# Transposed node table built before the main loop, and a new split of the gathered rows, in a graph message-passing kernel

## The chip, the cores and the metric

The kernel runs on one core of a Trainium2 chip. The metric is the time of one execution on the device, in microseconds (us). Five engines work side by side, each with its own queue of instructions: TensorE (PE in the profile, PEld for its weight loads), VectorE (DVE), ScalarE (ACT), GpSimd (POOL) and SyncE (SP), which here only issues DMA transfers. They wait for one another through semaphores.

## The reference

For 12500 nodes with 48 numbers each and 400000 edges (sorted by destination), one layer of message passing with a residual:

```python
h   = maximum(layernorm(x), 0)                    # [12500, 48]
tmp = concatenate([h[dst], h[src], edge_attr], 1) # [400000, 48 + 48 + 32]
msg = relu(tmp @ W1 + b1) @ W2 + b2               # [400000, 128] -> [400000, 48]
out = x + segment_sum(msg, dst, 12500)
```

The kernel never builds `tmp`. It forms two tables of node rows, `tab_a = h @ W1[:48] + b1` and `tab_b = h @ W1[48:96]`, both [12544, 128] in DRAM, and adds for each edge the row of its destination (from `tab_a`), the row of its source (from `tab_b`) and `edge_attr @ W1[96:]`. Since W2 is linear, the relu outputs are summed by destination first, and W2 is applied to the sums.

## The kernel before, in words

**Tiles and chunks.** 128 edges are a tile, 3125 tiles in all; 8 tiles (1024 edges) are a chunk, 391 chunks. Since edges are sorted by destination, the destinations of a chunk lie in a window of 80 nodes. 12 chunks share one accumulator of 1024 nodes in SBUF, a segment (`seg`, two of them in turn).

**Stage one, `node_tables`.** The node rows are loaded in six slices, normalised (DVE and ACT), transposed on PE into `ht` (features on partitions), and multiplied by the weights: first all of `tab_b`, then all of `tab_a`, each slice copied out of PSUM by ACT and DVE and stored by SP. Meanwhile POOL gathers the raw x rows of the source nodes of the first four chunks (`RAW = 4`; `gather`, line 760), because `tab_b` isn't ready that early; those rows are normalised too.

**Stage two, `windows`, the main loop.** The order of work on each engine is written out by hand (line 501 on). In iteration c:

- SP issues the loads of chunk c (`prepare`): edge attributes into `lhs` (line 354), the destinations broadcast over 80 partitions into `row` (356), the 80 rows of `tab_a` into `rhs` (364), whose address is first loaded into a register (272); then single rows of `tab_b` into `gs` (`rows`, line 289).
- POOL gathers source rows from `tab_b` by indirect DMA into `gb`, one tile of 128 rows an instruction (371). `gb` has 7 buffers.
- DVE compares `row` with the window's node numbers into the one-hot part of `lhs` (379), adds the sums of chunk c-2 to its segment (460), and builds the one-hot matrix `hot` (389).
- PE multiplies `lhs` by `rhs` for chunk c-1 (400), adds the source rows to it (421), and, for chunk c-2, sums the relu outputs by destination with `hot` (445).
- ACT does the relu of chunk c-1 (437).

**Three ways to a source row.** Not all source rows come through POOL. A second way are columns: `bt`, the table `tab_b` turned so that its 128 hidden values lie on partitions, stays in SBUF, and DVE and ACT copy one column of it per edge into `gt` (`columns`, line 348); PE turns `gt` back as it adds it. The addresses of the columns are loaded from SBUF into registers of the copying engine, in parts (`PARTS`; line 272). 143 columns a chunk are copied, 71 by DVE in five parts and 72 by ACT in six. The third way are the single rows that SP loads, 15 a chunk. As soon as 128 columns or rows are together they replace one of POOL's gathers.

**The turned table** `bt` is built in the first five chunks of the main loop (`turn`, lines 302 and 307): three blocks a chunk, each two products on PE and one copy on ACT. Columns therefore begin with chunk 5.

**Segments.** Every 12 chunks DVE copies the 80 overlapping nodes into the other segment and clears the rest of it (`segment_next`, 476 and 478); PE multiplies the finished segment by W2 in two blocks (488, 489), DVE adds it to x (495) and SP stores it (499), two chunks into the next segment. SP's store waits for DVE's addition, and everything SP issues behind it waits too.

Of the kernel before, what the change touches and what calls it, by code (L numbers as in the profile page):

```python
# [8 lines left out]
F32 = mybir.dt.float32  # L9
# [31 lines left out]
RAW = 4  # L41
NRAW = RAW * T
RAW_PART = 16
# [8 lines left out]
TURNS = 3  # L52
BLOCKS = (NPAD + CE - 1) // CE
BUILD = (BLOCKS + TURNS - 1) // TURNS
COLS = BUILD
# [10 lines left out]
STRIP = 144  # L66
# [3 lines left out]
RPART = 15  # L70
# [3 lines left out]
SEG0 = 161696  # L74
# [3 lines left out]
AT_PLACE, AT_SEG, SEG, NEXT = 16, 17, 18, 19  # L78
WIDTH = 20
# [10 lines left out]
BYCOLS = tiles_of(COLS, PART)  # L90
COLS_OF = {c: [j for j, of in enumerate(BYCOLS) if of == c] for c in sorted(set(BYCOLS))}
BYROWS = tiles_of(ROWS0, RPART)
EPS = 1e-5

# [7 lines left out]
def node_tables(nc, tc, keep, x, ident, w1, b1, wb, ht, xg, ones, tab_a, tab_b, index, loads,  # L102
                squares, most, check):

    slices = [(0, 8), (8, 16), (24, 20), (44, 20), (64, 20), (84, 14)]
# [6 lines left out]
    with ExitStack() as es:  # L112
        node = es.enter_context(tc.tile_pool(name="node", bufs=3))
        sqp = es.enter_context(tc.tile_pool(name="sqp", bufs=2))
        ps_t = es.enter_context(tc.tile_pool(name="ps_t", bufs=3, space=PSUM))
        ps_n = es.enter_context(tc.tile_pool(name="ps_n", bufs=3, space=PSUM))
# [5 lines left out]
        wa = keep.tile([2 * D + 1, 2, HID], F32, name="wa")  # L122
        nc.vector.memset(wb, 0.0)
# [21 lines left out]
        sqs = {}  # L145

        def centre(j):
            r0, rb = slices[j]
            h = xs[j]
            of = total[:, r0 : r0 + rb]  # L150
            nc.vector.tensor_reduce(of, h, AX.X, ALU.add)
            nc.vector.scalar_tensor_tensor(
                h, of.unsqueeze(2).to_broadcast([P, rb, D]), -1.0 / D, h,
                op0=ALU.mult, op1=ALU.add,
            )
            sqs[j] = sqp.tile([P, rb, D], F32, name="sq")
            nc.scalar.activation(sqs[j], h, AF.Square)

        def scale(j):
            r0, rb = slices[j]  # L160
            h = xs[j]
            of = rstd[:, r0 : r0 + rb]
            var = node.tile([P, rb], F32, name="var")
            nc.vector.tensor_reduce(var, sqs.pop(j), AX.X, ALU.add)
            std = node.tile([P, rb], F32, name="std")
            nc.scalar.activation(std, var, AF.Sqrt, bias=eps, scale=1.0 / D)
            nc.vector.reciprocal(of, std)
            nc.vector.tensor_mul(h, h, of.unsqueeze(2).to_broadcast([P, rb, D]))

        def turn(j):  # L170
            r0, rb = slices[j]
            h = xs[j]
            for g in range(0, rb // 2, 4):
                n = min(4, rb // 2 - g)
                p_t = ps_t.tile([2 * D, 4, P], F32, name="p_t")
                for q in range(n):
                    nc.tensor.transpose(
                        p_t[:, q, :],
                        h[:, 2 * (g + q) : 2 * (g + q) + 2, :].rearrange("p r d -> p (r d)"),
                        ident,  # L180
                    )
                nc.scalar.activation(
                    ht[: 2 * D, r0 // 2 + g : r0 // 2 + g + n, :], p_t[:, :n, :], AF.Relu
                )

        def table(j, wt, tv, dve):

            r0, rb = slices[j]
            rows = wt.shape[0]
            t = node.tile([P, rb, HID], F32, name="tab")  # L190
            for g in range(0, rb // 2, 2):
                n = min(2, rb // 2 - g)
                p_n = ps_n.tile([P, 2, 2 * HID], F32, name="p_n")
                for q in range(n):
                    nc.tensor.matmul(  # L195
                        p_n[:, q, :], ht[:rows, r0 // 2 + g + q, :],
                        wt.rearrange("k a h -> k (a h)"), start=True, stop=True,
                    )
                to = t[:, 2 * g : 2 * (g + n), :].rearrange("p r h -> p (r h)")
                of = p_n[:, :n, :].rearrange("p q h -> p (q h)")  # L200
                if dve and g % 4:
                    nc.vector.tensor_copy(to, of)
                else:
                    nc.scalar.copy(to, of)
            nc.sync.dma_start(tv[:, r0 : r0 + rb, :], t)

        for i in range(ns + 3):
            if i < ns:
                centre(i)
            if 0 <= i - 1 < ns:  # L210
                scale(i - 1)
            if 0 <= i - 2 < ns:
                turn(i - 2)
            if i == ns:
                squares()
            if i == ns + 1:
                most()
            if i == ns + 2:
                check()
            if 0 <= i - 3 < ns:  # L220
                table(i - 3, wb, tb_v, i >= ns)
        late = {1: (centre, ns), 2: (scale, ns), 3: (centre, ns + 1), 4: (scale, ns + 1)}
        for j in range(ns):
            if j in late:
                of, k = late[j]
                of(k)
            table(j, wa, ta_v, True)
# [707 lines left out]
```

## Time and profile before

| | |
|---|---|
| median of three runs | 3368.91 us |
| lowest, highest | 3366.3, 3372.81 us |
| profiled execution | 3372.65 us |
| its span | 3370.8 us |
| TensorE clock granted, mean | 0.911 |

The page of the profile gives, for one execution, the busy time of each engine, the chain of work that ended last, the costliest groups of instructions and the DMA traffic. "Issue" in it is time in which an engine waited for nothing that the profile shows. An instruction that only loads registers or issues a DMA isn't counted as busy; a `q` behind an engine's name (`SPq`, `DVEq`) marks such work of its queue. In the order of time each line has the start, the duration, the engine, the line of the code, what is written from what, and how many instructions are merged in it.

### The profile page before, as it was taken

The numbers are of one execution on the slowest core, as the hardware profiler recorded it, in microseconds if no ns is written. First come the engines' busy times: TensorE is split into PE (matmuls) and PEld (weight loads), VectorE is DVE, ScalarE is ACT, GpSimd is POOL, SyncE is SP. The second block draws the span as 40 slices with busy tenths as digits, with TensorE's granted clock in tenths as the row PEclk, the third lists the DMA queues.
The fourth block names the chain that finished last, engine by engine and source line by source line (L and its number), as shares of the span: only waits on it lengthen the run. The fifth ranks groups of instructions, "written<-read, shape, count | busy, mean of one in ns | idle before, by whom it ended". The sixth has DMA issues, their size and how long they took to land.

```text
span 3370.8 us, 115212 instructions
## 1 busy us (share of the span) xinstructions
PE 2775.6 (82%) x16394; PEld 2158.3 (64%) x16394; DVE 2800.1 (83%) x29140; ACT 3035.6 (90%) x28179; POOL 2530.0 (75%) x2670
## 2 busy tenths in 40 slices
PE   7987778888888888888887788888788788788777
PEld 6666666666666666666666666676666666666565
DVE  6588888888888888888888888888888888888876
ACT  5799998999998999998899999889998999999987
POOL 7677777777777777777777777777777777777776
PEclk9999998998898998988889999888998999899989
DMA  7433333333333333333333333333333333333333
GB/s 262 122 97 104 100 97 100 99 101 100 100 99 100 95 100 102 100 101 97 100 98 101 100 100 102 95 101 97 102 99 98 97 100 98 104 100 97 99 96 83
DMA packets 200234, 349.24 MB, mean 104 GB/s; under 512 B 69219, under 2 KB 107749, under 8 KB 198181
## 3 DMA queue, kind: packets, MB, share of 16 engines
q0 software_dynamic: 84800, 172.53, 18.9%
q1 hardware_dynamic: 114258, 169.09, 16.7%
q14 instruction: 634, 5.19, 0.5%
q8 instruction: 138, 2.26, 0.3%
q10 hardware_dynamic: 404, 0.17, 0.0%
HBM read 322.05 MB, written 22.07 MB: 102 GB/s over the span
## 4 chain that ended last, share of the span: by engine, by line
DVE 71%; issue 14%; PE 5%; DVEq 4%; POOL 2%; DMA 2%; ACT 0%; SPq 0%; POOLq 0%; ACTq 0%
DVE gt L348 47%; DVE lhs L379 12%; DVE hot L389 8%; DVEq L272 4%; DVE seg L460 2%; POOL gb L371 2%; PE pre L400 1%; PE p_g L445 1%; DVE xseg L495 1%; DVE seg L476 1%; DMA row<-in_dst 1%; PE p_f L488 1%; PE p_f L489 1%; DMA gb<-tab_b,srci 1%; PE p_n L195 1%
## 5 line engine op out<-in xcount | busy, mean ns | idle before, releaser
L371 POOL DMA_INDIRECT gb<-tab_b,srci x2618 | 2489.4, 951 | 812.7 <-issue 724.4
L348 ACT COPY gt<-bt 128x1 f32 x27705 | 2618.0, 188 | 63.9 <-issue 54.6
L348 DVE COPY gt<-bt 128x1 f32 x27335 | 1842.1, 144 | 463.3 <-issue 435.1
L400 PEld LDWEIGHTS pre<-rhs,lhs 112*128 112x128 f32 x6250 | 823.5, 208 | 277.1 <-issue 193.4
L400 PE MATMUL pre<-rhs,lhs 112*128 112x128 f32 x6250 | 841.5, 292 | 98.3 <-issue 56.7
L445 PE MATMUL p_g<-hot,hid 128*128 128x80 f32 x6250 | 794.0, 282 | 131.2 <-ACT hid L437 129.1
L445 PEld LDWEIGHTS p_g<-hot,hid 128*128 128x128 f32 x6250 | 758.4, 198 | 164.4 <-ACT hid L437 161.6
L421 PE MATMUL pre<-gb,ident 128*128 128x512 f32 (+2 forms) x1548 | 771.2, 627 | 34.3 <-DMA gb<-tab_b,srci 26.5
L437 ACT ACTIVATE hid<-pre 128x1024 f32<-128x1024 f32 x391 | 397.5, 1017 | 220.2 <-PE pre L421 205.8
L379 DVE TENSOR_SCALAR_CACHE_REDUCE lhs<-row,bw 80x1024 f32<-80x1024 int16 x391 | 494.6, 1265 | 14.8 <-DMA row<-in_dst 14.5
L421 PEld LDWEIGHTS pre<-gb,ident 128*128 128x128 f32 x1548 | 311.8, 225 | 281.0 <-issue 261.7
L421 PE MATMUL pre<-ident,gt 128*128 128x128 f32 x860 | 214.9, 336 | 261.7 <-DVE gt L348 234.7
L421 PEld LDWEIGHTS pre<-ident,gt 128*128 128x128 f32 x860 | 143.8, 210 | 291.5 <-issue 136.4
L389 DVE TENSOR_TENSOR hot<-wnum,rel 128x640 f32<-128x640 f32 x391 | 318.2, 814 | 0.0
L460 DVE TENSOR_TENSOR seg<-seg,p_g 128x160 f32 x391 | 121.5, 311 | 47.8 <-PE p_g L448 47.8
L448 PE MATMUL p_g<-ident,deg 80*128 80x80 f32 x782 | 156.4, 283 | 0.0
L448 PEld LDWEIGHTS p_g<-ident,deg 80*128 80x128 f32 x782 | 123.6, 198 | 0.0
L488 PE MATMUL p_f<-seg,w2s 128*48 128x512 f32 (+1 forms) x134 | 82.2, 700 | 44.3 <-DVE xseg L495 43.9
L489 PE MATMUL p_f<-seg,b2s 1*48 1x512 f32 (+1 forms) x134 | 76.2, 650 | 0.0
L488 PEld LDWEIGHTS p_f<-seg,w2s 128*48 128x48 f32 x134 | 12.3, 135 | 85.9 <-DVE xseg L495 60.0
L476 DVE MEMSET seg<- 128x944 f32 x64 | 54.1, 845 | 9.3
L489 PEld LDWEIGHTS p_f<-seg,b2s 1*48 1x48 f32 x134 | 11.3, 122 | 65.2 <-issue 65.2
(76 smaller groups left out, 429.0 us busy)
## 6 DMA issues: line engine op xcount, KB each, us to landing
gs<-tab_b SPq DMA_DIRECT2D x5760, 0.5 KB
row<-in_dst SPq DMA_DIRECT2D x390, 160.0 KB
lhs<-in_edge_t SPq DMA_DIRECT2D x390, 128.0 KB
gb<-tab_b,srci POOLq DMA_INDIRECT x2618
rhs<-tab_a SPq DMA_DIRECT2D x391, 40.0 KB
xseg<-in_x_t SPq DMA_DIRECT2D x33, 192.0 KB
out_x<-xseg SPq DMA_DIRECT2D x33, 192.0 KB
tab_b<-tab SPq DMA_DIRECT2D x3, 1280.0 KB
```

Of the source, the lines that this page charges most:

```text
L272: return nc.values_load_multi_w_load_instructions(table[c % P : c % P + 1, c // P, at : at + n], engines=[engine], min_val=0, max_val=1 << 23,
L348: copy(gts[j][:, e : e + 1], bt8[:, bass.ds(of, 4)].bitcast(F32))
L371: nc.gpsimd.indirect_dma_start(out=gb[:, t, :], out_offset=None, in_=tab_b[:, :], in_offset=bass.IndirectOffsetOnAxis(ap=srci[:, c * T + t ...
L379: nc.vector.tensor_scalar(lhs[:W, : n * P], row[:, : n * P], bw[:, c : c + 1], None, op0=ALU.is_equal, op1=ALU.add, accum_out=deg[:, :1],)
L389: nc.vector.tensor_tensor(hot[:, :n, :], wnum.unsqueeze(1).to_broadcast([P, n, W]), rel[:, c * T : c * T + n].unsqueeze(2).to_broadcast([P ...
L400: nc.tensor.matmul(pre[:, t, :], s["lhs"][:K, t * P : (t + 1) * P], s["rhs"][:K, :], start=t % BANK == 0, stop=False, skip_group_check=True,)
L421: nc.tensor.matmul(pre[:, t:e, :], lhsT, rhs, start=False, stop=True, skip_group_check=True)
L437: nc.scalar.activation(h[:, :n, :], s["pre"][:, :n, :], AF.Relu)
L445: nc.tensor.matmul(p_g[:, 0, :], s["h"][:, t, :], s["hot"][:, t, :], start=t == 0, stop=t == n - 1)
L448: nc.tensor.matmul(p_g[:, 1, :], s["deg"], ident[:W, :W], start=True, stop=True)
L460: nc.vector.tensor_add(to, to, s["p_g"])
L488: nc.tensor.matmul(p_f[:, :n], w2s, seg[:, 0, s], start=True, stop=False)
```

## The change

Seven things change together.

1. `bt` is built in stage one, for each slice before its rows of `tab_b` (`turned`); the rows of `tab_b` are then transposes of `bt` on PE, copied mostly by DVE (`back`). `tab_a` still comes from products with `ht` (`product`). The steps of a slice are cut into small functions and interleaved with the normalisation (`together`). `turn` is gone from the main loop, and `ht` lives in stage one alone.
2. A column of `bt` now stands at `(node mod 98) * 128 + node // 98`, the order in which the blocks come out, so the addresses are worked out in more DVE operations (`addresses`).
3. Five chunks use raw x rows (`RAW = 5`): 40 early gathers instead of 32. Columns begin in iteration 4.
4. 72 columns a chunk on DVE, in four parts of 23, 16, 17 and 16; 76 on ACT, in five parts; 17 single rows on SP. The place of the sums is loaded with the first part.
5. The segments are cleared by a DMA from a block of zeros, issued by SP behind the store of the segment (`segment_clear`), not by DVE.
6. `gb` has 8 buffers instead of 7.
7. The check that no edge lies outside its window uses a maximum and a minimum on DVE instead of squares on ACT; small operations for it move from POOL to DVE.

```diff
-RAW = 4
+RAW = 5
-RAW_PART = 16
+RAW_PART = 20
+RAW_EARLY = 16
-COLS = BUILD
+COLS = RAW - 1
 PARTS = (
-    (True, 0, 8), (True, 8, 15), (True, 24, 16), (True, 40, 20), (True, 60, 12),
-    (False, 72, 12), (False, 84, 8), (False, 92, 8), (False, 100, 20), (False, 120, 12),
-    (False, 132, 12),
+    (True, 0, 23), (True, 24, 16), (True, 40, 17), (True, 60, 16),
+    (False, 76, 12), (False, 88, 16), (False, 104, 20), (False, 124, 12), (False, 136, 16),
 )
-RPART = 15
+RPART = 17
...
+        def turned(j, g):
 
             r0, rb = slices[j]
+            n, at = min(2, rb // 2 - g), r0 // 2 + g
+            p_b = ps_n.tile([P, 4 * HID], F32, name="p_b")
+            parts = p_b[:, : 2 * n * P].rearrange("h (k q p) -> h k q p", k=2, q=n)
+            for k in range(2):
+                nc.tensor.matmul(
+                    parts[:, k, :, :].rearrange("h q p -> h (q p)"), wb[:, k, :],
+                    ht[: 2 * D, at : at + n, :].rearrange("k g p -> k (g p)"),
+                    start=True, stop=True,
+                )
+            nc.scalar.copy(
+                bt[:, 2 * at * P : 2 * (at + n) * P].rearrange("h (q k p) -> h q k p", k=2, q=n),
+                parts.rearrange("h k q p -> h q k p"),
+            )
+
+        def back(j, g):
+
+            r0, rb = slices[j]
+            n = min(4, rb - 2 * g)
+            if g == 0:
+                tabs[j] = node.tile([P, rb, HID], F32, name="tab")
+            p_n = ps_n.tile([P, 4 * HID], F32, name="p_n")
+            for q in range(n):
+                at = (r0 + 2 * g + q) * P
+                nc.tensor.transpose(p_n[:, q * HID : (q + 1) * HID], bt[:, at : at + P], ident)
+            copy = nc.scalar.copy if j >= ns // 2 and g % 6 == 4 else nc.vector.tensor_copy
+            copy(tabs[j][:, 2 * g : 2 * g + n, :].rearrange("p r h -> p (r h)"), p_n[:, : n * HID])
+            if 2 * g + n == rb:
+                nc.sync.dma_start(tb_v[:, r0 : r0 + rb, :], tabs.pop(j))
...
-        def turn(i):
-
-            n = min(T, NR - i * T)
-            p_t = ps_p.tile([P, T, HID], F32, name="pre")
-            parts = p_t.rearrange("h (k q) p -> h k q p", k=2)
...
         def segment_next(g):
 
             old, new = segs[g % 2], segs[(g + 1) % 2]
-            if g > 0:
-                for k in range(2):
-                    nc.vector.memset(new[:, k, W:], 0.0)
...
+        def segment_clear(g):
+
+            nc.sync.dma_start(segs[g % 2][:, :, W:], zeros.unsqueeze(0).to_broadcast([P, 2, L - W]))
...
                 if g > 0 and k == STORE:
                     segment_store(g - 1, L)
+                    if begin(g + 1) < NCH:
+                        segment_clear(g - 1)
...
-                for i in range(c * TURNS, min((c + 1) * TURNS, BLOCKS)):
-                    turn(i)
...
-    gp = ctx.enter_context(tc.tile_pool(name="gp", bufs=7))
+    gp = ctx.enter_context(tc.tile_pool(name="gp", bufs=8))
...
+            def lanes():
+                nc.vector.tensor_scalar(
+                    at, cols, 1.0 / NR, 0.5 / NR - 0.5, op0=ALU.mult, op1=ALU.add
+                )
+                nc.vector.tensor_scalar_add(at, at, ROUND)
+
+            def whole():
+                nc.vector.tensor_scalar(
+                    at, at, -ROUND, 4.0 - 4.0 * NR * P, op0=ALU.add, op1=ALU.mult
+                )
+                nc.vector.tensor_scalar_add(at, at, float(BT0))
+
+            def turned_places():
+                nc.vector.scalar_tensor_tensor(
+                    cols, cols, 4.0 * P, at, op0=ALU.mult, op1=ALU.add
+                )
+                nc.vector.tensor_scalar_add(at_place, place, float(BT0))
```

More of the change, by code (lines that the diff above doesn't have):

```diff
@@ L93 @@
 EPS = 1e-5
+ROUND = 1.5 * 2**23
 G = 5
@@ L99, with node_tables @@
 GNACC = 4
-def node_tables(nc, tc, keep, x, ident, w1, b1, wb, ht, xg, ones, tab_a, tab_b, index, loads,
-                squares, most, check):
-    slices = [(0, 8), (8, 16), (24, 20), (44, 20), (64, 20), (84, 14)]
+def node_tables(nc, tc, keep, x, ident, w1, b1, bt, wb, xg, ones, tab_a, tab_b, index, loads,
+                flags, check, addresses):
+    slices = [(0, 8)] + [(r0, 18) for r0 in range(8, NR, 18)]
     ns = len(slices)
@@ L188, in table @@
+        def turned(j, g):
             r0, rb = slices[j]
[L189 to L204, printed above, removed]
@@ L210, in node_tables @@
             if 0 <= i - 1 < ns:
[L211 to L227, printed above, removed]
+                side += scale(i - 1)
@@ new lines, in node_tables @@
+            if i >= ns:
+                side += later[i - ns]
+            main = [lambda g=g: turn(i - 2, g) for g in groups(i - 2, 4)]
+            t, b = groups(i - 3, 2), groups(i - 4, 2)
+            for k in range(max(len(t), len(b))):
+                if k < len(t):
+                    main.append(lambda g=t[k]: turned(i - 3, g))
+                if k < len(b):
+                    main.append(lambda g=b[k]: back(i - 4, g))
+            if main:
+                together(main, side)
+            else:
+                for do in side:
+                    do()
@@ L522, in windows @@
                     nc.vector.memset(segs[c], 0.0)
+                columns(c, 2)
                 columns(c, 3)
```

250 lines of the change are left out of this document (143 added, 107 removed).

## The prediction

> **What bounds the kernel now.** I read the page's parts 1, 4 and 5 first, then the waits of each engine, then the order of time in the steady part. On the page no engine is idle enough to be ruled out:
>
> ```profile
> span 3370.8 us, 115212 instructions
> PE 2775.6 (82%) x16394; PEld 2158.3 (64%) x16394; DVE 2800.1 (83%) x29140; ACT 3035.6 (90%) x28179; POOL 2530.0 (75%) x2670
> ...
> DVE 71%; issue 14%; PE 5%; DVEq 4%; POOL 2%; DMA 2%; ACT 0%; SPq 0%; POOLq 0%; ACTq 0%
> ...
> L371 POOL DMA_INDIRECT gb<-tab_b,srci x2618 | 2489.4, 951 | 812.7 <-issue 724.4
> L348 ACT COPY gt<-bt 128x1 f32 x27705 | 2618.0, 188 | 63.9 <-issue 54.6
> L348 DVE COPY gt<-bt 128x1 f32 x27335 | 1842.1, 144 | 463.3 <-issue 435.1
> ...
> L476 DVE MEMSET seg<- 128x944 f32 x64 | 54.1, 845 | 9.3
> ```
>
> The busy shares mislead. POOL is 75% busy, but with its issue time it is full: a gather starts every 1.25 us to the end (3349.74, 3350.98, 3352.23), and it waited for a buffer only once for long.
>
> ```profile
> 3349.74 0.94 POOL L371 DMA_INDIRECT gb<-tab_b,srci  x1 [0.30 <-issue]
> 3350.98 0.94 POOL L371 DMA_INDIRECT gb<-tab_b,srci  x1 [0.30 <-issue]
> 3352.23 0.94 POOL L371 DMA_INDIRECT gb<-tab_b,srci  x1 [0.30 <-issue]
> ...
> POOL gb L371 <- PE pre L421: 13.0, 1, 13.0
> ```
>
> The chain runs through DVE, 71%, with 14% "issue". Those gaps stand where DVE's queue loads column addresses into registers (line 272): the shortest load, of 8 values, takes 598 ns and the longest, of 20, 1352, so 63 ns a value. DVE begins its compare of line 379 once a chunk:
>
> ```profile
> L379 DVE TENSOR_SCALAR_CACHE_REDUCE lhs<-row,bw x287: 1259/1266/1276, 601.3 to 2995.0; 80x1024 f32<-80x1024 int16 x144
> ...
> L272 DVEq TENSOR_LOAD <-cols x7: 598/1100/1352, 2004.2 to 2013.3; - x7
> L272 SPq TENSOR_LOAD <-last x2: 557/862/1168, 2006.0 to 2012.6; - x2
> ```
>
> (2995.0 - 601.3) / 286 = 8.37 us a chunk. POOL needs 8 - (143 + 15) / 128 = 6.77 gathers a chunk, 8.46 us, and has a lead from the start. The two are level.
>
> SP does not appear in part 1, as issuing DMAs is not counted as busy. Yet its queue is a fourth loop of almost the same length. From the order of time on SP:
>
> ```profile
> 1068.32 0.33 SPq L354 DMA_DIRECT2D lhs<-in_edge_t  x1
> 1068.70 0.41 SPq L356 DMA_DIRECT2D row<-in_dst  x1
> 1070.47 0.33 SPq L364 DMA_DIRECT2D rhs<-tab_a  x1
> 1070.90 4.81 SPq L289 DMA_DIRECT2D gs<-tab_b  x15
> 1075.82 0.33 SPq L354 DMA_DIRECT2D lhs<-in_edge_t  x1
> ...
> 1137.97 0.33 SPq L354 DMA_DIRECT2D lhs<-in_edge_t  x1
> 1138.34 0.41 SPq L356 DMA_DIRECT2D row<-in_dst  x1
> 1140.08 0.33 SPq L364 DMA_DIRECT2D rhs<-tab_a  x1
> 1140.53 5.18 SPq L289 DMA_DIRECT2D gs<-tab_b  x15
> 1156.59 0.35 SPq L499 DMA_DIRECT2D out_x<-xseg  x1
> 1157.04 0.37 SPq L354 DMA_DIRECT2D lhs<-in_edge_t  x1
> ...
> SPq L499 <- DVE seg L460: 153.4, 24, 12.0
> SPq L499 <- DVE xseg L495: 50.7, 8, 9.2
> ```
>
> A chunk takes SP 1075.82 - 1068.32 = 7.50 us without a pause, of which 15 single-row loads are 4.81. Its only real rest is once per segment of 12 chunks, before the store at line 499, where it waits for DVE. The last two rows are SP's waits between 140 and 3300 us: 153.4 + 50.7 = 204.1 us in 32 waits, **6.4 us a segment**. That is all the room SP has, and it cannot run ahead past a store.
>
> **The change, part by part.**
>
> *Rows on SP, 15 to 17 a chunk.* A row costs (4.81 - 0.23) / 14 = 0.327 us of SP (15 starts, the last ends 0.23 after its start). There are 45 x 128 = 5760 rows now and 51 x 128 = 6528 then: 768 more, 24 in a segment, 7.8 us. SP also loads 18 addresses instead of 16 at line 272. In the rows above one value took 557 ns and 16 took 1168, 41 ns each; DVE's 63 is the other bound. That is 0.08 to 0.13 us a chunk, 1.0 to 1.5 us a segment; I take 1.1, as the first is SP's own.
>
> ```profile
> L469 SPq DMA_DIRECT2D xseg<-in_x_t x34: 320/329/334, 96.8 to 3331.0; - x34
> ...
> L771 SPq DMA_DIRECT2D cols<-in_src_strip x1: 929/929/929, 9.4 to 9.4; - x1
> ...
> q1 hardware_dynamic: 114258, 169.09, 16.7%
> ```
>
> The Trainium skill, Runtime: NRT & Kernel Launch, section "Instruction fetch mechanics", puts a register load at about 200 ns a register. By that the two values would cost 0.4 us a chunk, some 120 us over the run more than I take; the 41 ns above disagree, and the sum goes by them.
>
> *The clear as a DMA.* It takes the two memsets per segment off DVE: 64 x 0.845 = 54 us. It puts on SP one issue per segment, behind the store, of 128 partitions x 2 pieces of 3776 bytes. No row shows such an issue: 48 pieces took 329 ns, 128 took 929 once. Bounds 0.33 to 1.9 us (two of the latter), I take 0.7. What it waits for (PE's reads of the sums) is done before the store's own wait ends, so no new wait; what stands behind it on SP is the next chunk's lhs, row and rhs. Its 0.97 MB go through the hardware queue, which moved 169.09 MB in 16.7% of 16 engines' span, 300 GB/s: 3.2 us, which the next row load can be late by. If SP is the slower one, DVE has about 3 us of room in a segment, which covers it; without cover 32 x 3.2 = 100 us. I take 0, and this case stands as rival C.
>
> *SP's sum.* 7.8 + 1.1 + 0.7 = 9.6 us more in a segment, against 6.4 us of rest. SP runs out: 3.2 us a segment. The pauses that stretch its loop now (5.18 for 15 rows at 1140.53 instead of 4.81) grow with the instructions, 24 of 250: 0.3 us. So **3.5 us a segment, 32 segments, 112 us**. Bounds: 7.8 + 1.0 + 0.33 - 6.4 = 2.7, 87 us; with 1.5 and 1.9, 4.8, 154 us. If every pause of SP vanished, its segment would still be 12 x (7.50 + 0.65 + 0.08) + 2.3 for the load and store + 0.7 = 101.8 us against 12 x 8.37 = 100.4 now: 1.4 us, 45 us.
>
> *Columns: 71 to 72 on DVE, 72 to 76 on ACT.* ACT: 4 x 2618.0 / 27705 = 0.38 us a chunk, 146 us in all, into ACT's waits for PE:
>
> ```profile
> ACT hid L437 <- PE pre L421: 190.8, 125, 8.5
> ...
> L795 POOL TENSOR_SCALAR off<-off 128x16 f32<-128x16 f32 x1 | 0.3, 258 | 0.1
> ```
>
> It fits, with little left; cost 0, and if the cover were gone, up to 146. DVE: the loads change from 8, 16, 16, 20, 12 values to 24, 16, 20, 16: by 63 ns a value and 94 a load 4.99 becomes 5.16 us, +0.16; one copy more, +0.07; the memset gone, -54.1 / 391 = -0.14. Together +0.09 us a chunk, 35 us, if the queue sets DVE's pace; -0.07, a gain of 27, if the engine does. Under SP's pace this is hidden: 35 us is less than 112.
>
> *Gathers.* POOL's tiles are 3125 - 32 - 430 - 45 = 2618 now and 3125 - 40 - 446 - 51 = 2588 then. With 40 instead of 32 early x rows that is 22 fewer, 22 x 1.25 = 27.5 us; the five small operations at lines 792 to 796 that move from POOL to DVE save at most 1.3 (the longest, line 795, has 0.26); I take 1.1. The eighth gather buffer and earlier columns can remove the 13.0 us stall. All of it is worth nothing while POOL's consumers are slower than POOL: the wait for a buffer comes back late in the run.
>
> *The start.* The turned table leaves the first five chunks and enters the stage before them:
>
> ```profile
> L195 PE MATMUL p_n<-wb,ht 96*128 96x256 f32 x98 | 25.3, 414 | 0.5 <-ACT tab L204 0.5
> L307 ACT COPY bt<-pre 128x1024 f32<-128x1024 f32 x12 | 24.3, 2101 | 3.5 <-PE pre L302 3.5
> L302 PE MATMUL pre<-ht,wb 96*128 96x512 f32 x48 | 23.3, 624 | 5.3 <-ACT bt L307 5.3
> ...
> L204 ACT COPY tab<-p_n 128x512 f32<-128x512 f32 x33 | 18.7, 585 | 12.6 <-PE p_n L195 12.3 <-ACT ht L182 0.2
> L202 DVE COPY tab<-p_n 128x512 f32<-128x512 f32 (+1 forms) x17 | 11.1, 658 | 10.4 <-PE p_n L195 10.4
> ...
> L177 PE MATMUL p_t<-ident,xs 128*96 128x128 f32 x49 | 8.8, 339 | 13.0 <-DVE xs L168 13.0
> ...
> L354 SPq DMA_DIRECT2D lhs<-in_edge_t x9: 327/520/568, 74.9 to 133.7; - x9
> ```
>
> The 25.3 us of table matmuls stay, over the same columns, now giving the turned table. Added are 98 transposes at 8.8 / 49 = 0.18, 17.6 us of PE, and some 25 copies at 0.6 on ACT and on DVE each. Removed from the first chunks are 23.3 us on PE and 24.3 on ACT. The longer address work is five DVE operations of under 1 us. Between -20 (all removed work was on the path, the additions fill idle time) and +20 (the reverse) I take 0.
>
> *Sum against the profiled execution*, 3372.65 us (3370.8 span and 1.85 around it): 3372.65 + 112 - 0 = 3485. That execution lies 3.7 us over the median of the three runs, so **3480 us** for a median.
>
> **The rivals.**
>
> *A. SP's issues stay hidden; POOL sets the pace: faster.* Mechanism: the new issues fill the 6.4 us rest. It decides below 6.4 us a segment, that is if a row costs under (6.4 - 1.8) / 24 = 0.19 us. Then 27.5 + 1.1 + 13.0 come off: 3372.65 - 41.6 - 3.7, 3327 us. For it: POOL never rests. Against it: 0.327 us a row over 15 rows in a line, and DVE's longer loads, which alone would take most of it back. The Trainium skill, DMA: Bandwidth & Descriptors, section "Issuing engines are not separate DMA queues", says the time to initiate a DMA is usually small beside the DMA; by it the 768 issues would cost nothing and A would hold. The rows disagree, since 15 issues of 0.5 KB fill 4.81 of 7.50 us. 8%.
>
> *B. DVE's register loads set the pace.* SP's pauses shrink and the rows fit nearly; DVE then gives +35, SP without pauses +45: some 3372.65 + 40 - 3.7, 3409 us. 9%.
>
> *C. The clears hold up the row loads.* Up to 3.2 us a segment on top of SP's: 3540 to 3580. For it: one row load follows each clear at once. Against it: DVE has 3.5 us of room in a segment. 6%.
>
> *D. Nothing measurable*: rests and gains cancel, within 7 us of 3369. 3%.
>
> **How the numbers follow.** SP as the pace has 74%, with its own range 3440 to 3535 (87 to 154 us, with the start at -12 and +12). Adding B makes 83%: the range is 3390 to 3540. Leaving 0.2% (7 us) as the least that a measurement of this kernel tells from no change: faster 0.09 (A and a part of B's gain side), same 0.03, slower 0.88.
>
> **What the changed profile would show.** SP's chunk at 8.2 us without a pause, 17 rows in about 5.45 us; the waits at line 499 nearly gone; DVE waiting for the row loads, which it hardly does now; POOL waiting for buffers from the middle of the run on; ACT's wait for PE not smaller. The start shows as the first lhs load, now at 74.9 us, later by about 10, and faster chunks behind it. I am wrong if SP still waits some us for DVE at the stores: then its rows were cheaper or its loop had more air. I am wrong in the other way if DVE's gaps at the copies grow by more than 0.2 us a chunk with SP still resting.

## The result, and the profile after

| | before | after |
|---|---|---|
| median of the runs | 3370.06 us (3366.3 to 3372.81) | 3731.85 us (3723.07 to 3735.34) |
| ratio, 95% interval | | 1.107 [1.1048, 1.1093] |
| profiled execution | 3372.65 us | 3735.34 us |
| span | 3370.8 us | 3733.5 us |

The changed kernel is 10.7% slower, 362 us. The forecast was slower, 3480 us, with SP's queue as the new pace. The pace is SP's, but the loss is three times the forecast one.

The page of the changed kernel, parts 1, 4, 5 and 6:

```profile
span 3733.5 us, 118510 instructions
PE 2908.1 (78%) x16502; PEld 2281.9 (61%) x16502; DVE 2802.4 (75%) x29567; ACT 3224.7 (86%) x29769; POOL 2490.1 (67%) x2643
...
SPq 34%; DVE 18%; ACT 13%; issue 12%; PE 10%; DMA 9%; DVEq 1%; ACTq 1%
SPq L350 20%; DVE gt L391 12%; ACT gt L391 12%; SPq L333 8%; DMA row<-in_dst 7%; PE pre L464 4%; DVE lhs L422 3%; PE pre L443 3%; SPq L397 2%; SPq L399 2%; ACT hid L480 2%; DVE hot L432 2%; PE p_g L488 2%; SPq L407 2%; DMA rhs<-tab_a 1%
...
L414 POOL DMA_INDIRECT gb<-tab_b,srci x2588 | 2443.5, 944 | 1157.9 <-issue 726.8
L391 ACT COPY gt<-bt 128x1 f32 x29296 | 2831.7, 187 | 126.8 <-issue 84.9
L391 DVE COPY gt<-bt 128x1 f32 x27792 | 1836.8, 144 | 604.7 <-issue 569.6
...
L422 DVE TENSOR_SCALAR_CACHE_REDUCE lhs<-row,bw 80x1024 f32<-80x1024 int16 x391 | 495.5, 1267 | 272.9 <-DMA row<-in_dst 267.8
...
seg<-in_zeros SPq DMA_DIRECT2D x32, 944.0 KB
```

No engine's busy time fills the 363 us that the span grew: DVE has 2802.4 us (2800.1 before), POOL 2490.1 (2530.0), ACT 3224.7 (3035.6, four columns more a chunk) and PE 2908.1 (2775.6; its granted clock is 0.867 after 0.911). So all of them wait more. The chain says for whom: SP's queue has 34% of it, where it had 0%, and the row loads (`DMA row<-in_dst`) 7%. In SP's part stand the 17 single-row loads (line 350, 20%) and the loads of addresses into registers (line 333, 8%). The compare of line 422 costs the same 1267 ns, but DVE stood 272.9 us idle before it.

The waits of the changed kernel between 140 and 3700 us (total us, times, longest):

```profile
SPq L350 <- DMA seg<-in_zeros: 101.7, 32, 4.1
SPq L350 <- DMA row<-in_dst: 17.0, 31, 1.3
...
DVE lhs L422 <- DMA row<-in_dst: 251.3, 79, 8.3
...
POOL gb L414 <- PE pre L464: 393.4, 140, 9.0
...
ACT hid L480 <- PE pre L464: 285.6, 105, 7.7
```

The same view of the kernel before has, for DVE and POOL between 140 and 3300 us:

```profile
DVE lhs L379 <- DMA row<-in_dst: 2.1, 5, 0.9
...
POOL gb L371 <- PE pre L421: 16.1, 49, 1.5
```

SP's 204.1 us of waits for DVE at the store are gone altogether: no row for line 543 is left. DVE now waits for the row loads (251.3 us after 2.1), and POOL, which never rested, waits for buffers (393.4 after 16.1). The first row is the one that the prediction does not have: SP itself stops for the DMA that clears the segment, 101.7 / 32 = 3.2 us each time. The second row, too, comes 31 times, about once a segment.

SP in order of time, the changed kernel, around an ordinary chunk and around a store (start us, duration us):

```profile
1077.36 0.33 SPq L397 DMA_DIRECT2D lhs<-in_edge_t  x1
1077.74 0.41 SPq L399 DMA_DIRECT2D row<-in_dst  x1
1079.93 0.33 SPq L407 DMA_DIRECT2D rhs<-tab_a  x1
1080.35 5.45 SPq L350 DMA_DIRECT2D gs<-tab_b  x17
1085.91 0.33 SPq L397 DMA_DIRECT2D lhs<-in_edge_t  x1
...
1159.73 5.79 SPq L350 DMA_DIRECT2D gs<-tab_b  x17
1166.36 0.34 SPq L543 DMA_DIRECT2D out_x<-xseg  x1
1166.80 0.41 SPq L524 DMA_DIRECT2D seg<-in_zeros  x1
1167.27 0.66 SPq L397 DMA_DIRECT2D lhs<-in_edge_t  x1
1167.99 0.46 SPq L399 DMA_DIRECT2D row<-in_dst  x1
1170.04 0.33 SPq L407 DMA_DIRECT2D rhs<-tab_a  x1
1170.48 9.19 SPq L350 DMA_DIRECT2D gs<-tab_b  x17
1179.78 0.33 SPq L397 DMA_DIRECT2D lhs<-in_edge_t  x1
```

An undisturbed chunk takes SP 1085.91 - 1077.36 = 8.55 us (7.50 before). Behind the store (line 543) follows the clear (line 524); its issue takes 0.41 us. Then the next 17 single rows take 9.19 us instead of 5.45. DVE at the same place:

```profile
1168.00 1.06 DVE L391 COPY gt<-bt 128x1 f32 x16 [0.66 <-issue]
...
1176.23 1.27 DVE L422 TENSOR_SCALAR_CACHE_REDUCE lhs<-row,bw 80x1024 f32<-80x1024 int16 x1 [7.17 <-DMA row<-in_dst]
...
1185.11 1.27 DVE L422 TENSOR_SCALAR_CACHE_REDUCE lhs<-row,bw 80x1024 f32<-80x1024 int16 x1
```

The row load issued at 1167.99, the second load behind the clear, was there only at 1176.2, and DVE waited 7.17 us for it. By the landings in the trace, the row load of the chunk behind a clear takes 8.5 us from issue to landing in the median, the others 3.0: it is 5.4 us late. The clear itself takes 8.2 us.

From the starts of the compare in the traces I worked out the mean step from one compare to the next by its place in the segment of 12 chunks (chunks 20 to 380). Place 2 is the step in which SP issues the store, place 9 the one in which it issues the load of the next block of x, place 11 the one with the change of segment.

| kernel | mean of all chunks, us | most places | place 2 | place 9 | place 11 |
|---|---|---|---|---|---|
| before | 8.38 | 8.1 to 8.4 | 9.4 | as most | 9.4 |
| after | 9.30 | 8.35 to 8.75 | 15.4 | 10.5 | 9.3 |

So 6.0 of the (9.30 - 8.38) x 12 = 11.0 us that a segment lost stand at place 2, 2.3 at place 9, and the rest is spread over the ordinary steps. 377 chunks of 0.917 us are 346 us; the remaining 15 lie ahead of compare 13, which starts at 205.0 us instead of 189.6.

### The profile page after: what moved, and what is told of

Read it like the earlier page. It is cut to its first block, busy times and chain, and to the rows that moved or that the text cites. A ratio compares the mean times of both kernels' runs of the same rounds, so it can differ in the third digit from the quotient of the medians.

```text
span 3733.5 us, 118510 instructions
## 1 busy us (share of the span) xinstructions
PE 2908.1 (78%) x16502; PEld 2281.9 (61%) x16502; DVE 2802.4 (75%) x29567; ACT 3224.7 (86%) x29769; POOL 2490.1 (67%) x2643
## 4 chain that ended last, share of the span: by engine, by line
SPq 34%; DVE 18%; ACT 13%; issue 12%; PE 10%; DMA 9%; DVEq 1%; ACTq 1%
SPq L350 20%; DVE gt L391 12%; ACT gt L391 12%; SPq L333 8%; DMA row<-in_dst 7%; PE pre L464 4%; DVE lhs L422 3%; PE pre L443 3%; SPq L397 2%; SPq L399 2%; ACT hid L480 2%; DVE hot L432 2%; PE p_g L488 2%; SPq L407 2%; DMA rhs<-tab_a 1%
## 5 line engine op out<-in xcount | busy, mean ns | idle before, releaser
L414 POOL DMA_INDIRECT gb<-tab_b,srci x2588 | 2443.5, 944 | 1157.9 <-issue 726.8
L391 ACT COPY gt<-bt 128x1 f32 x29296 | 2831.7, 187 | 126.8 <-issue 84.9
L443 PEld LDWEIGHTS pre<-rhs,lhs 112*128 112x128 f32 x6250 | 879.0, 220 | 452.6 <-issue 380.0
L443 PE MATMUL pre<-rhs,lhs 112*128 112x128 f32 x6250 | 904.5, 306 | 264.0 <-DVE lhs L422 243.7
L488 PE MATMUL p_g<-hot,hid 128*128 128x80 f32 x6250 | 819.8, 288 | 145.2 <-ACT hid L480 144.5
L488 PEld LDWEIGHTS p_g<-hot,hid 128*128 128x128 f32 x6250 | 790.3, 205 | 170.8 <-ACT hid L480 169.3
L464 PE MATMUL pre<-gb,ident 128*128 128x512 f32 (+3 forms) x1544 | 793.7, 647 | 0.0
L422 DVE TENSOR_SCALAR_CACHE_REDUCE lhs<-row,bw 80x1024 f32<-80x1024 int16 x391 | 495.5, 1267 | 272.9 <-DMA row<-in_dst 267.8
L464 PE MATMUL pre<-ident,gt 128*128 128x128 f32 x892 | 233.6, 352 | 342.7 <-DVE gt L391 294.4
L464 PEld LDWEIGHTS pre<-gb,ident 128*128 128x128 f32 x1544 | 327.1, 235 | 254.3 <-issue 246.5
L539 DVE TENSOR_TENSOR xseg<-xseg,p_f 48x512 f32<-48x512 f32 (+1 forms) x67 | 44.6, 666 | 8.9 <-PE p_f L533 8.9
```

The costliest lines, as they stand in the source:

```text
L391: copy(gts[j][:, e : e + 1], bt8[:, bass.ds(of, 4)].bitcast(F32))
L414: nc.gpsimd.indirect_dma_start(out=gb[:, t, :], out_offset=None, in_=tab_b[:, :], in_offset=bass.IndirectOffsetOnAxis(ap=srci[:, c * T + t ...
L422: nc.vector.tensor_scalar(lhs[:W, : n * P], row[:, : n * P], bw[:, c : c + 1], None, op0=ALU.is_equal, op1=ALU.add, accum_out=deg[:, :1],)
L443: nc.tensor.matmul(pre[:, t, :], s["lhs"][:K, t * P : (t + 1) * P], s["rhs"][:K, :], start=t % BANK == 0, stop=False, skip_group_check=True,)
L464: nc.tensor.matmul(pre[:, t:e, :], lhsT, rhs, start=False, stop=True, skip_group_check=True)
L488: nc.tensor.matmul(p_g[:, 0, :], s["h"][:, t, :], s["hot"][:, t, :], start=t == 0, stop=t == n - 1)
```

## The experiments

Theory S: SP's queue is the pace, and the loss is made of SP's own instructions. Rival C, as in the prediction: the clear as a DMA holds up what stands behind it. Rival P: DVE's and ACT's new division of the columns is itself too long, and shows as soon as SP is relieved. The expectations name two more: V, DVE's queue with its longer register loads sets the pace, and T, the new start and the new order of the columns cost the time. Behind each measured median stands its ratio to the kernel before, run beside it, with the 95% interval. Some diffs show only the lines that matter; `...` marks what is left out.

### One part undone in the changed kernel

The first runs take back one part each, or do one part alone in the kernel before. The 15 rows in the changed kernel:

```diff
-RPART = 17
+RPART = 15
```

> The changed kernel with 15 single rows a chunk instead of 17 (and so 16 addresses in SP's load instead of 18); all else stays. Theory S (SP's queue sets the pace of the changed kernel): 24 rows of 0.327 us and 12 address loads of 1.61 instead of 1.18 us leave SP's segment, 7.8 + 5.1 = 12.9 us of 111.7; SP then rests again and DVE or the late row loads behind the clear set the pace: 3440 to 3550 us. Rival V (DVE's queue with its longer register loads sets the pace): nothing leaves DVE, 3700 to 3735. Rival T (the new start and the new order of columns): also 3700 or more.

Measured 3574.09 us, 1.0618 [1.0601, 1.0636]: two rows less take off 158 us of 364, so V and T, by which nothing would have gone, cannot hold most of the loss. The time lies 24 us above the range expected of S. The waits (140 to 3540 us):

```profile
SPq L543 <- DVE seg L503: 197.9, 26, 9.7
SPq L350 <- DMA seg<-in_zeros: 111.7, 32, 4.6
...
DVE lhs L422 <- DMA row<-in_dst: 130.9, 28, 6.0
```

SP rests again at the store, 197.9 us and more, as before the change. Yet the kernel is 206 us slower than before, and DVE still waits 130.9 us for row loads. With SP resting, S alone cannot explain that; the chain of this run is 59% DVE and 6% row loads, and only 2% SP's queue. Place 2 of the segment takes 13.6 us here, all other steps at most 9.2.

The memset of DVE put back, the DMA clear taken out, 17 rows kept:

```diff
+            if g > 0:
+                for k in range(2):
+                    nc.vector.memset(new[:, k, W:], 0.0)
...
-                    if begin(g + 1) < NCH:
-                        segment_clear(g - 1)
```

> The changed kernel with the segments cleared by DVE again, no clear on SP. Theory S: the issue (0.41 us) and the stall of the ninth transfer behind it (3.7 us) leave SP, 4.1 us a segment over 32 segments: 3733 - 131 = about 3600 us. Rival V: DVE gets 54 us of memsets back, so 3730 to 3790. Rival T: no change.

Measured 3601.3 us, 1.0695 [1.0677, 1.0713]: 131 us are the clear's. Place 2 falls from 15.4 to 9.75 us; place 9 stays at 10.5. SP does not rest here: between 140 and 3300 us it waited 0.6 us at the store. So what is left, 233 us over the kernel before, is mostly the loss by SP's own instructions; the next run has them alone. The waits for row loads behind the clear are gone with it, 17.0 us before:

```profile
SPq L350 <- DMA row<-in_dst: 0.2, 1, 0.2
```

The rows alone, in the kernel before (17 rows, with the table of addresses widened from 20 to 24 entries to hold two more):

```diff
-RPART = 15
+RPART = 17
...
-AT_PLACE, AT_SEG, SEG, NEXT = 16, 17, 18, 19
-WIDTH = 20
+AT_PLACE, AT_SEG, SEG, NEXT = 20, 21, 22, 23
+WIDTH = 24
```

> The kernel before with 17 single rows a chunk instead of 15 alone. Theory S: SP's segment goes from 94.5 us of work to 94.5 + 7.8 + 5.1 = 107.4, 8.95 us a chunk against 8.38 now: 3370 + 377 x 0.57 = about 3585 us. Rivals V and T, in which SP isn't what limits: POOL has 45 x 128 / 128 tiles less by 6, so 3360 to 3370 us.

Measured 3581.74 us, 1.0631 [1.0614, 1.0649]: 213 us from two rows a chunk and nothing else. By the prediction's prices they should have cost 7.8 + 1.1 - 6.4 = 2.5 us a segment, 80 us. A step of this kernel takes 8.93 us in the mean, and a step of the changed kernel without the clear, which has the new columns besides, 8.94: under SP's pace the columns cost nothing more. Its waits (140 to 3300 us) and SP's load of addresses between 2000 and 2020 us (x2: min/median/max ns):

```profile
SPq L499 <- DVE seg L460: 6.7, 1, 6.7
...
DVE lhs L379 <- DMA row<-in_dst: 131.6, 128, 3.1
```

```profile
L272 SPq TENSOR_LOAD <-last x2: 1657/1658/1660, 2004.3 to 2013.4; - x2
```

The load of 18 addresses takes 1.66 us. The kernel before takes 1186 ns in the median for 16 and the kernel after 1610 for 18 (the rows of all loads; the shortest are those of one address for store and x block):

```profile
L272 SPq TENSOR_LOAD <-last x459: 274/1186/1317, 75.8 to 3363.4; - x153
```

```profile
L333 SPq TENSOR_LOAD <-last x459: 277/1610/1680, 89.2 to 3726.1; - x153
```

0.42 us for two values, where the prediction had 0.08 to 0.13. With 0.42 x 12 = 5.1 us for the addresses, two rows a chunk cost 7.8 + 5.1 - 6.4 = 6.5 us a segment, 208 us, and 213 were measured. From the loads on DVE and SP in these traces the duration seems to go by whole groups of four: 8 values 0.60 us, 16 1.12 to 1.18, 20 1.38, 24 1.64; 18 take 1.62 to 1.66, as much as 24. That fits some 0.11 us, and 0.25 for each group of four or each single value left over: 18 would be four groups and two singles, six loads. (Loads of one value alone, 0.27 to 0.6 us on SP, follow it only roughly.) This gave an experiment: load 20 and use 18.

```diff
-            base, *nodes = numbers(c, BASE, 1 + m, mybir.EngineType.SP)
+            base, *nodes = numbers(c, BASE, -(-(1 + m) // 4) * 4, mybir.EngineType.SP)[: 1 + m]
```

> The changed kernel, SP's address load reads 20 values instead of 18 (two unused). If a load costs by the value (41 to 63 ns), it gets longer by 0.1 us a chunk: about 3770 us. If it costs by groups of four with the odd ones taken singly (16: 1.12, 20: 1.38, 24 and 18: 1.63 us in the changed trace), it gets shorter by 0.25 us a chunk, and by theory S the kernel by 390 x 0.25 = 97: about 3635 us. Rivals V and T: no change.

Measured 3657.7 us, 1.086 [1.0842, 1.0878]: loading two addresses more made the changed kernel 74 us faster, 0.19 us a chunk; 97 were expected. SP's loads between 2000 and 2020 us, among them one of a few addresses (584):

```profile
L333 SPq TENSOR_LOAD <-last x4: 584/1334/1438, 1999.1 to 2018.3; - x4
```

Over the whole run SP's load of 20 takes 1.42 us in the median, that of 18 1.62: 0.20 us a chunk, as measured. The sign rules out one price per value, by which the kernel would have become slower. That four is the group, and that odd values go singly, rests on the durations alone.

### Where the clear's price comes from

The clear is issued five places later in the segment, at k = 7, with 15 rows:

```diff
-RPART = 17
+RPART = 15
...
+                if g > 0 and k == 7 and begin(g + 1) < NCH:
+                    segment_clear(g - 1)
...
-                    if begin(g + 1) < NCH:
-                        segment_clear(g - 1)
```

> The changed kernel with 15 rows and the clear issued seven chunks into the segment (five chunks after the store) instead of right behind the store; the same bytes, the same issue. The run with 15 rows alone had 13.6 us for the chunk behind the store (9.4 in the kernel before) and 8.4 for an ordinary one. Theory S2 (the clear hurts only because SP has no lead over DVE behind the store, so the next row load lands late): the 13.6 falls to about 9.2, 4.3 us a segment, 32 segments: 3574 - 138 = about 3435 us. Rival (the clear's traffic slows whatever runs beside it): the 4 us come back in the chunks that then follow the clear, 3560 to 3580.

Measured 3437.86 us, 1.0205 [1.0188, 1.0222]: the same 32 clears of the same bytes cost 136 us less than behind the store. SP's waits (140 to 3380 us):

```profile
SPq L543 <- DVE seg L503: 107.2, 25, 7.4
SPq L350 <- DMA seg<-in_zeros: 55.3, 31, 2.6
...
DVE lhs L422 <- DMA row<-in_dst: 11.1, 13, 1.5
```

SP still stops for the clear (55.3 us), but DVE waits for row loads only 11.1 us, not 130.9: at the seventh place SP is ahead and the late row load has time. The row load behind the clear is late here too, 7.0 us from issue to landing instead of 3.1. Behind the store SP has just come out of its wait for DVE and has no lead; there the next row load is wanted at once. So the price is not the bytes and not the issue, but the place.

With the memset back and 15 rows:

```diff
-RPART = 17
+RPART = 15
...
+            if g > 0:
+                for k in range(2):
+                    nc.vector.memset(new[:, k, W:], 0.0)
...
-                    if begin(g + 1) < NCH:
-                        segment_clear(g - 1)
```

> The changed kernel with 15 rows and DVE's memsets instead of the clear: nothing of SP's is left. If DVE's own queue then sets the pace at 8.4 us for an ordinary chunk (8.15 before), with 9.4 at the store and 9.5 at the change of segment: 8.57 a chunk, 198 + 377 x 8.57 + 22 = about 3450 us. If the parts, the start and the order of columns cost nothing, 3350 to 3380.

Measured 3431.45 us, 1.0182 [1.016, 1.0203]: 143 us below the 15 rows alone, and 6 below the clear at the seventh place. The clear costs 4.5 us a segment here, against 131 / 32 = 4.1 with 17 rows.

And the clear alone, in the kernel before (with `segment_clear` and the block of zeros as in the change):

```diff
-            if g > 0:
-                for k in range(2):
-                    nc.vector.memset(new[:, k, W:], 0.0)
...
+                    if begin(g + 1) < NCH:
+                        segment_clear(g - 1)
```

> The kernel before with the clear as a DMA behind the store alone. SP has room for the issue and the stall (4.1 of 6.4 us). If rests were all that counts, DVE is rid of 54 us of memsets: 3315 to 3370 us. If the row load behind the clear lands late, the chunk behind the store gets 4.2 us longer and the change of segment 1.5 to 2 shorter: 32 x 2.4, about 3370 + 77 = 3445 us.

Measured 3503.54 us, 1.04 [1.0382, 1.0417], 58 us more than I expected. Its waits (140 to 3300 us):

```profile
SPq L500 <- DVE seg L460: 103.2, 19, 9.9
SPq L500 <- DVE xseg L496: 57.6, 12, 6.2
SPq L289 <- DMA seg<-in_zeros: 114.2, 30, 4.8
...
DVE lhs L379 <- DMA row<-in_dst: 124.0, 29, 6.3
```

SP still has 160.8 us of rest, and the kernel loses 135 us all the same. Place 2 grows by 4.5 us, and the memset's removal gives only 0.5 back at place 11. I had expected a late row load of under 4 us and most of the memsets' 54 us.

Why SP stops at the single rows: in the trace each DMA of SP's queue uses the semaphore of the eighth before it, so the eighth DMA behind the clear takes over the clear's semaphore. Around 1170 us in the changed kernel that is a single row: the one before it is issued at 1171.5 us, it itself only at 1174.6. In all 32 segments of each of the five kernels with a clear (the changed one, 20 addresses, 15 rows, the clear at the seventh place, the clear alone), this eighth DMA is issued 15 to 17 ns after the last part of the clear has landed. That it is the semaphore and not another limit of the queue is read from these numbers; no run changes it. What makes the transfers behind the clear land late is not shown by a run either.

### What is left: the columns, and the start

The division of the columns alone, in the kernel before, with 71 columns on DVE in four parts, 76 on ACT in five, and the calls of `columns` in the new order:

```diff
-    (True, 0, 8), (True, 8, 15), (True, 24, 16), (True, 40, 20), (True, 60, 12),
-    (False, 72, 12), (False, 84, 8), (False, 92, 8), (False, 100, 20), (False, 120, 12),
-    (False, 132, 12),
+    (True, 0, 23), (True, 24, 16), (True, 40, 16), (True, 56, 16),
+    (False, 72, 12), (False, 84, 16), (False, 100, 20), (False, 120, 12), (False, 132, 16),
...
```

> The kernel before with DVE's 71 columns in four parts of 23, 16, 16, 16 (loads of 24, 16, 16, 16 values) in the order of the changed kernel, and 76 columns on ACT; 15 rows, memsets on DVE. If DVE's pace is the sum of its loads and copies: 18 groups of four as before, one load less, 0.1 us a chunk off; POOL has 12 gathers less. POOL then limits: 3370 - 13 to 3370 - 28, 3342 to 3357 us. If ACT is at its limit with 76: 3400 or more.

Measured 3409.4 us, 1.0118 [1.0101, 1.0135], 41 us. The page's groups for ACT:

```profile
L347 ACT COPY gt<-bt 128x1 f32 x29241 | 2825.0, 188 | 100.3 <-issue 58.9
...
L436 ACT ACTIVATE hid<-pre 128x1024 f32<-128x1024 f32 x391 | 396.2, 1013 | 30.5 <-PE pre L420 16.1
```

ACT's wait for PE, 205.8 us on the page before, is down to 16.1, and the chain of this run is ACT's:

```profile
ACT 78%; PE 8%; ACTq 5%; DVE 4%; issue 4%; DVEq 1%; DMA 0%; POOL 0%; SPq 0%
```

So ACT is the pace here, and the cover that the prediction named is gone. And points 1, 2, 3, 6 and 7 of the change without the rest (the changed kernel with the old parts in their old order, 15 rows and the memsets):

```diff
-    (True, 0, 23), (True, 24, 16), (True, 40, 17), (True, 60, 16),
-    (False, 76, 12), (False, 88, 16), (False, 104, 20), (False, 124, 12), (False, 136, 16),
+    (True, 0, 8), (True, 8, 15), (True, 24, 16), (True, 40, 20), (True, 60, 12),
+    (False, 72, 12), (False, 84, 8), (False, 92, 8), (False, 100, 20), (False, 120, 12),
+    (False, 132, 12),
...
-RPART = 17
+RPART = 15
...
+            if g > 0:
+                for k in range(2):
+                    nc.vector.memset(new[:, k, W:], 0.0)
...
-                    if begin(g + 1) < NCH:
-                        segment_clear(g - 1)
```

> The changed kernel with the old parts (71 columns on DVE in five, 72 on ACT in six, in the old order), 15 rows and memsets: what stays of the change is the turned table in the first stage, five chunks of x rows, the new addresses, the eighth buffer and the check. If all loss came from SP's queue, the clear and the parts: 8.38 us a chunk again, with a start 6 us later (DVE's compare of chunk 13 at 195 instead of 190 us): 3370 to 3380 us. If the new start or the new order of columns costs more: 3390 and up. If the buffer and the fewer gathers help: 3350.

Measured 3374.94 us, 1.0021 [1.001, 1.0033]: 7 us. In the profiled execution, with 3368.37 us one of the fastest of the seven, compare 13 starts 3.4 us later than in the kernel before. The parts, put in one after the other (the steps add up to the whole by construction):

| put in, from the kernel before on | median, us | step |
|---|---|---|
| nothing | 3368 | |
| start, addresses, buffer, check of the windows | 3375 | +7 |
| the columns' division, 72 and 76 | 3431 | +56 |
| the clear as a DMA behind the store | 3574 | +143 |
| two rows a chunk more | 3732 | +158 |

The steps hold for this order. In the kernel before, each alone, the columns cost 41, the clear 135 and the rows 213 us: what the rows and the columns take depends on the rest that the other parts have left to SP and ACT.

Is it the 76 columns on ACT, or the parts? In the kernel before, ACT's last two parts 16 and 12 instead of 12, six parts as they were, 76 in all:

```diff
-    (False, 72, 12), (False, 84, 8), (False, 92, 8), (False, 100, 20), (False, 120, 12),
-    (False, 132, 12),
+    (False, 72, 12), (False, 84, 8), (False, 92, 8), (False, 100, 20), (False, 120, 16),
+    (False, 136, 12),
...
```

> The kernel before with 76 columns on ACT instead of 72 alone (one part of 12 becomes 16). Theory (ACT's loop of 76 copies of 0.097 us, the relu of 1.0 and gaps of 0.15 is 8.5 us a chunk, over DVE's 8.38): 3395 to 3415 us, as in the run with both engines' parts changed. Rival (it was DVE's four parts): 3355 to 3370 us.

Measured 3365.73 us, 0.9997 [0.9981, 1.0012]: the theory that 76 are too many falls. The same two rows of its page:

```profile
L348 ACT COPY gt<-bt 128x1 f32 x29241 | 2794.1, 187 | 48.4 <-issue 34.7
...
L437 ACT ACTIVATE hid<-pre 128x1024 f32<-128x1024 f32 x391 | 396.1, 1013 | 67.3 <-PE pre L421 50.2
```

The same 29241 copies take 2794.1 + 48.4 = 2842.5 us with their idle time, in five parts 2825.0 + 100.3 = 2925.3: 97.2 against 100.0 ns a column, 83 us in all. ACT is the pace with five parts and has 50.2 us of waits for PE left with six. The two kernels differ in DVE's parts too, so that the number of parts on ACT does it is likely, not shown. The two kernels that follow have five parts on ACT and four on DVE as well, and 99.6 and 100.4 ns a column.

Now DVE's four parts with ACT at 72 and at 74 columns, in the kernel before (the same division with a last ACT part of 12 and of 14):

```diff
+    (True, 0, 23), (True, 24, 16), (True, 40, 16), (True, 56, 16),
+    (False, 72, 12), (False, 84, 16), (False, 100, 20), (False, 120, 12), (False, 132, 12),
...
```

> The kernel before with DVE's 71 columns in four parts (loads of 24, 16, 16, 16 values) and ACT's 72 in five. DVE has one load and one break less, about 0.1 us a chunk; ACT has the same 72. Theory: DVE leaves the path, POOL with 6.77 gathers of 1.25 us sets the end: 3350 to 3362 us. Rival (DVE's breaks only move): 3365 to 3375 us.

Measured 3364.25 us, 0.9992 [0.9983, 1.0001]: no gain that can be told; it lies in neither of the ranges expected.

```diff
-    (False, 72, 12), (False, 84, 16), (False, 100, 20), (False, 120, 12), (False, 132, 12),
+    (False, 72, 12), (False, 84, 16), (False, 100, 20), (False, 120, 12), (False, 132, 14),
```

> The same with 74 columns on ACT: ACT's loop is 74 x 0.097 + 1.0 + 0.15 = 8.3 us, POOL's 8.44. Theory: POOL sets the end with 6 gathers less, 3343 to 3358 us; rival (ACT's loop stretches by its waits as with 76): 3370 to 3390 us.

Measured 3357.94 us, 0.9969 [0.9956, 0.9982], 0.3% faster than the kernel before and 6 us faster than the one with 72. POOL's and ACT's groups on its page:

```profile
L370 POOL DMA_INDIRECT gb<-tab_b,srci x2612 | 2478.4, 949 | 813.4 <-issue 752.7
L347 ACT COPY gt<-bt 128x1 f32 x28473 | 2755.1, 188 | 104.8 <-issue 58.6
```

PE's waits (140 to 3300 us):

```profile
PE pre L420 <- DMA gb<-tab_b,srci: 60.7, 40, 4.0
```

Most of DVE's steps are 8.0 to 8.3 us here, ACT's copies with their idle time 2859.9 us, between the 2681.9 of the kernel before and the 2925.3 of 76 in five parts, and PE waits for POOL's gathers (28.3 us in the same window before). Two columns a chunk more replace 6 gathers, 2612 instead of 2618, at 1.25 us 7.5 us; 3364.25 - 3357.94 = 6.3 were measured. The one combination here that gained anything, 10 us, is DVE's four parts with half of ACT's addition.

## Why the prediction was right or wrong

**Direction and mechanism: right.** "SP runs out": its rests at the store, 204.1 us, are gone, DVE waits for rows, POOL for buffers, and SP has 34% of the chain. The rows' own price was right too: 17 in (5.45 - 0.23) / 16 = 0.326 us each, and with them 24 x 0.326 = 7.8 us a segment as forecast. The signs listed came, with two off: SP's chunk without a pause is 8.55 us, not 8.2, and the difference is the address load; and POOL waits for buffers from the start (54.4 us between 140 and 600 us already), not from the middle of the run on.

**The size: wrong, in two terms of "SP's sum".** Forecast 3.5 us a segment; measured 11.0.

| term, us a segment | forecast | measured |
|---|---|---|
| 24 single rows | 7.8 | 7.8 |
| 18 addresses instead of 16 | 1.1 | (1.61 - 1.19) x 12 = 5.1 |
| issue of the clear | 0.7 | 0.4 |
| SP's stop for the clear | 0 ("no new wait") | 3.2 |
| other pauses | 0.3 | about 0.5: waits for row, rhs and lhs transfers rose from about 12 to 30 us, most of it behind the clear |
| SP's rest | -6.4 | -6.4 |
| sum | 3.5 | 10.6 |

The sum leaves out the columns, which SP's pace hides; it accounts for 10.6 of the 11.0 us. Its three terms for the clear, 0.4 + 3.2 + 0.5, are the 131 / 32 = 4.1 us that the run without it gained.

The first failed step is the price of the two added addresses. It came from two durations of one row, 557 and 1168 ns, read as a line through 1 and 16 values, although all the larger sizes in sight were multiples of four and 18 is not. The two odd values cost (1.61 - 1.19) / 2 = 0.21 us each. The Trainium skill, Runtime: NRT & Kernel Launch, section "Instruction fetch mechanics", puts a load at about 200 ns a register, for loads from HBM; the prediction gave its result, 120 us, and set it aside for 41 ns. For the two odd values this price is near, though the addresses lie in SBUF here; in groups of four the trace has 63 ns a value, so it does not hold there.

The second is "so no new wait" and, with it, the cover taken for rival C. The prediction asked what the clear waits for and what stands behind it on the queue, not what its own landing holds up: the eighth DMA behind it, which uses its semaphore again. And C was priced as 3.2 us of transfer, covered by 3.5 us of DVE's room. (That SP's stop measures 3.2 us as well is chance: it is another quantity.) The clear took 8.2 us to land, the row load behind it was 5.4 us late, and the cover argument fails twice: where SP rests (15 rows) it has just waited for DVE, so there is no lead at that place; where it does not rest (17 rows) the stop adds to SP's own path. C had 6% and 3540 to 3580 us; its mechanism was real, and cost 131 to 143 us in three pairs of runs.

**The rivals.** A (SP's issues hidden) fell at its own condition, 0.19 us a row against 0.326. The Trainium skill, DMA: Bandwidth & Descriptors, section "Issuing engines are not separate DMA queues", calls the time to initiate a DMA usually small beside the DMA. For these loads of 0.5 KB it is about a quarter, 0.326 us beside a median of 1.4 us from issue to landing in the trace, and on a queue that sets the pace two more a chunk, with their addresses, cost 6.3%. B (the register loads of DVE set the pace) is not what happened. With SP relieved, the division of the columns costs 41 to 56 us, but not by DVE's loads alone: in the first of these runs the chain is 78% ACT, in the second 54% DVE and 23% ACT.

**The columns.** DVE's +0.16 and +0.07 us a chunk were about right: its shortest mean steps are 8.35 us instead of 8.10. ACT's "cost 0, and if the cover were gone, up to 146" was right under SP's pace; ACT's wait for PE is not smaller but larger, 285.6 us. Not foreseen: the same columns are dearer in the kernels with five parts on ACT than in those with six.

**The start.** Taken as 0, with -12 to +12. Alone it is 7 us with all else that is left in that run, inside these bounds; the first chunks behind the start were faster, as forecast, since the first lhs load of that run came 12.4 us later and compare 13 only 3.4. In the changed kernel the first lhs load came 12.7 us later than its 74.9, where some 10 were forecast (its loads of lhs up to 140 us; first and last start at the end):

```profile
L397 SPq DMA_DIRECT2D lhs<-in_edge_t x7: 338/528/660, 87.6 to 132.7; - x7
```

**The range.** Its upper end, 3540, came from bounds on terms that I had: 0.08 to 0.13 us for the addresses and 0.33 to 1.9 for the clear's issue. The first did not hold its term, 0.42, because it was drawn between two prices per value. The second held the issue, 0.4, but the sum had no term for the stop, and so no bound.

## What to carry to other kernels

An engine whose work is issuing DMAs has a loop of its own that the busy shares do not show; before work is put on it, its rest in a period is to be read from its waits, and every instruction priced at the exact count that it will have, also the loads of addresses. A large transfer in a queue of small ones is to be asked where its landing is waited for, and issued where the queue is ahead of its consumers, not directly behind a wait for them. And a cover counts only at the place where it is needed: 6.4 us of rest a segment did not help a load that was wanted at the very end of that rest.

## What the runs showed of the hardware that was not expected

- A load of 18 addresses into SP's registers took longer than one of 20: 1.19 us in the median for 16, 1.62 for 18, 1.42 for 20. Loading two unused values more was worth 74 us in 3732.
- A 944 KB clear in a line of small DMAs stopped its queue for 3.2 us, at the eighth DMA behind it, and made the 160 KB load behind it land 5.4 us late; its place alone decided over 136 us.
- 29241 one-column copies on ACT took 97.2 ns each with their idle time in six parts and 100.0 in five. The cause is open.
